# Sums of values over both key chunks in one visit of TensorE, with a re-measured planner

## The chip, the cores and the metric

The kernel runs on one core of a Trainium2 chip. Its engines are TensorE (PE in the profile; its weight loads are PEld), VectorE (DVE), ScalarE (ACT), GpSimd (POOL) and SyncE (SP), which issues all DMAs here. The metric is the device time of one execution in microseconds; a figure for a kernel is the median of its runs.

## The reference

Four transformer blocks follow each other on x, 16 batches of 256 tokens of width 256, with a context of 77 tokens a batch and a conditioning vector a batch. All is in fp32, with 16 heads of width 16.

```python
x = L0(x, cond, ctx, masks)   # adaLN, rope, masked self-attention, masked cross-attention, GELU MLP of 1024
x = L1(x, ctx, cond)          # adaLN on x and on ctx, cross-attention
x = L2(x, cond, ctx)          # adaLN, self-attention, cross-attention, MLP
x = L3(x, cond, ctx)          # adaLN, rope, self-attention, cross-attention, MLP

def attn(q, k, v, mask):      # in all of them
    s = einsum('bqhd,bkhd->bhqk', q, k) * scale      # masked in L0
    return einsum('bhqk,bkhd->bqhd', softmax(s), v)
```

So there are three self-attentions (256 keys, two chunks of 128), four cross-attentions (77 keys, one chunk) and three MLPs, each over 16 batches.

## The kernel before

**Stages.** All of x stays in SBUF. The work comes in stages: attention of L0 ("a" self, "ac" cross), its MLP ("b"), attention of L1 and L2 ("cx", "c", "cc"), its MLP ("d"), attention of L3 ("e", "ec"), its MLP ("f"). Within a stage the batches overlap in a wave: a batch's cross-attention starts 16 places behind its self-attention.

**One attention** (`attention`, L757). x is normed (`norm_tasks`: statistics on VectorE, scaling on POOL), turned through DRAM (a VectorE transpose of 32x32 blocks, L539, a DMA out, a DMA in) into xT; the first BY_PE = 2 batches of the masked attention are turned on TensorE instead (L518). Projections (`strips`, L639) cut the array into four column strips, 128 rows by 32 columns each. Heads lie in pairs of 32 rows: scores cut the array into four row strips, 32 by 128. There are two rounds of scores. In the first (L872 with 256 keys, L884 with 77) queries are on the partitions and VectorE takes each row's maximum from PSUM (L902, L906; for the masked self-attention with the mask added, L898; for the first BY_PE batches the mask is added by a bf16 matmul, L863). The maxima go through DRAM into the queries as extra rows. In the second round (L965, L958 the masks) keys are on the partitions; ScalarE takes the exponential of each bank (L979, L977) into a buffer "ec" of four row strips. One half (g) of the heads and one chunk (kc) of 128 keys fill one such buffer with four exponentials. Then `values` (L983, matmul L988) multiplies them with v in four column strips: eight matmuls a chunk, two visits of the array for a half in self-attention, both into one PSUM bank, which the first visit takes. v's tile holds 64 columns for a pair of heads, of which values fill two quarters and ones the other two, so that the same matmul sums the exponentials. The sums are turned by VectorE (L997), inverted (L1004), multiplied in by POOL (L1010), turned back (L1014) and projected (L639 again) onto x.

**The MLP** (`mlp`, L1065). Per batch eight blocks of 128 hidden units, two full-array matmuls each (L1087), GELU on ScalarE (L1092) into an "ec" buffer, and L1038 back. GELU and exponential need different function tables on ScalarE.

**Context.** `context_T` (L591) loads the context in ten tiles, norms it for L1 and L2, and turns it on TensorE (L626) into a buffer "ctx" of [2, 1232] columns. There are two such buffers; at the start one holds the bf16 masks. For L1, `scale1` (L1250) applies the modulation "1k" to the whole context on VectorE. A modulation (`modulation`, L379) loads weights into a "kq" buffer, multiplies (L389), turns (L400) and adds.

**Order.** Nothing is ordered by hand. Each step is a Task with an engine, an estimated duration, dependences, and the buffers (Hold) it takes and uses; CAPS says how many of each there are (8 PSUM banks "b", 2 "ec", 2 "ctx", 5 "kq", ...). `Order.solve` (L102) plays a list schedule on these estimates and returns the order in which the steps are issued. An engine takes the ready step of the least priority value (TensorE) or the longest ready one (the others); a result is taken to reach another engine LAG = 0.13 us after the step's end; a change between row strips and others costs 0.2 or 0.13 us (TURN). Two score steps of opposite halves of the rows (rp 0 and 1) are issued interleaved, so that all four row strips run; `choose` (L151) pairs them. Only the order depends on these estimates; on the chip the engines wait for semaphores.

The planner's constants and its one call, before:

```python
    LAG = 0.13                                                                   # L77
    u.ready = max(u.ready, t.end + (self.LAG if u.eng != t.eng else 0.0))        # L199
    for ts in od.solve():                                                        # L1302
```

Of the kernel before, what the change touches and what calls it, by code (L numbers as in the profile page):

```python
# [17 lines left out]
P = 128  # L18
# [55 lines left out]
class Order:  # L74


    LAG = 0.13  # L77
# [8 lines left out]
    def add(self, eng, dur, run, deps=(), take=(), use=(), prio=0, rp=None, kind=None, more=0.0,  # L86
            lat=0.0, first=False, mb=0.0):

        t = Task()
        t.more, t.lat, t.first, t.mb = more, lat, first, mb  # L90
# [9 lines left out]
        return t  # L100

    def solve(self, seed=0):  # L102
# [65 lines left out]
        while n_done < len(self.tasks):  # L168
# [19 lines left out]
            assert nxt, "no step can start"  # L188
            now = min(nxt)
            while events and events[0][0] <= now + 1e-9:  # L190
                _, _, t = heapq.heappop(events)
                n_done += 1
                for h in t.held:
                    h.users -= 1
                    if not h.users:
                        loose[h.tag].append(h.no)
                for u in t.outs:
                    u.left -= 1
                    u.ready = max(u.ready, t.end + (self.LAG if u.eng != t.eng else 0.0))  # L199
                    if not u.left:  # L200
                        waiting.setdefault(u.eng, []).append(u)
# [4 lines left out]
def pixart_kernel(ctx: ExitStack, tc: tile.TileContext, x, cond_t, ctx_in, mask_c, mask_s, tables, vecs, rows,  # L206
# [7 lines left out]
    CAPS = {"b": 8, "xn": 1, "xT": 2, "kq": 5, "v": 5, "mx": 3, "mr": 2, "ec": 2,  # L214
            "ts": 2, "oT": 2, "rope": 2, "qk": 4, "tmp": 2, "gb": 3, "wa": 1, "ctx": 2,
# [3 lines left out]
    wpool = ctx.enter_context(tc.tile_pool(name="weights", bufs=1))  # L219
# [5 lines left out]
    SHAPES = {"kq": [2, 2, 512], "v": [NT, H, 32], "xn": [NT, D], "xT": [NC, N], "y": [4, NT * NC * 32],  # L225
# [36 lines left out]
    h_mask = Hold("ctx")  # L262
# [31 lines left out]
    BY_PE = 2  # L294
# [5 lines left out]
    def ones_out():  # L300
        for m in mrs:
            nc.sync.dma_start(m[1].rearrange("s r n -> r s n"),
                              vs[-1][0:4].rearrange("r t h w -> r (t h w)").rearrange("r (s n) -> r s n", n=512))
    ones_t = add("POOL", 3.2, ones, prio=3)
# [34 lines left out]
    sc_t = add("DVE", 0.6, silu, deps=[t], prio=200)  # L339


    def load_weights(src, block, deps=(), prio=-1):
# [12 lines left out]
        h, views, tasks, s = Hold("wa"), {}, {}, {}  # L355

        def open_w():
            s["w"] = wpool.tile([P, WMAX], F32, tag="wa", name=f"w_{block}")
        t0 = add("NO", 0.0, open_w, deps=deps, take=[h], prio=prio)
        names, off = [], 0  # L360
        for name, cols in BLOCKS[block]:
            if name not in ("qr", "kr", "cqr", "ckr"):
                names.append((name, off, NC * cols))
            off += NC * cols

        def load(name, off, n):
            w = s["w"][:, off:off + n]
            nc.sync.dma_start(w, src[:, off:off + n])
            views[name] = w.rearrange("p (c n) -> p c n", c=NC)
        for i, (name, off, n) in enumerate(names):  # L370
            tasks[name] = add("SP", ISSUE, lambda name=name, off=off, n=n: load(name, off, n), deps=[t0],
# [123 lines left out]
    def norm_tasks(s, b, eps, mod, name, prio, deps=(), direct=False):  # L495
# [31 lines left out]
        t1 = add("DVE", 1.0, stats, deps=[x_done[b], *deps], take=[hs], prio=prio)  # L527
        t2 = add("POOL", 0.95, rstd, deps=[t1], use=[hs], prio=prio)
        t3 = add("POOL", 2.5, scale, deps=[t2], take=[hn], use=[hs], prio=prio)
# [32 lines left out]
        t = add("DVE", 0.75, turn32, deps=[t3], take=[hy], use=[hn], prio=prio)  # L562
# [28 lines left out]
    def context_T(name, eps, prio, deps=()):  # L591
# [6 lines left out]
        for j in range(0, CT, P):  # L598
# [7 lines left out]
            if eps is not None:  # L606
# [11 lines left out]
                t = add("DVE", 0.5, stats, deps=[t], take=[hs], use=[hi], prio=prio)  # L618
                t = add("POOL", 0.95, rstd, deps=[t], use=[hs], prio=prio)
# [31 lines left out]
    def take_q(s, bias, src, a, use, prio):  # L651
# [8 lines left out]
        return add("ACT", 1.1 if bias is None else 1.25, run, deps=[a], use=use, prio=prio)  # L660

    def take_k(s, bias, n, src, a, use, prio):
# [15 lines left out]
        d = (0.6 if big else 0.33) if bias is None else (0.95 if big else 0.5)  # L678
# [3 lines left out]
    def rotate_tasks(s, key, ws, xT, src_t, n, half, uses, name, prio):  # L682
# [6 lines left out]
        for group in ([list(range(nt))] if len(ws) == 1 else [[t] for t in range(nt)]):  # L689
# [44 lines left out]
            d = add("POOL", 0.65 * size, sines, deps=[a, tab_t], take=[hr], use=[hq], prio=prio)  # L734
# [22 lines left out]
    def attention(b, name, n, wv, wkeys, h_w, w_t, eps, mod, half, biases, masked, pre_add, gate, prio, ctxs=None,  # L757
# [7 lines left out]
        h_masks = [h_mask] if masked else []  # L765
# [68 lines left out]
        def take_v():  # L834
            pv = uv["p"][0:rows_n, 0:nk * D].rearrange("p (t h w) -> p t h w", h=H, w=HD)
            pairs = s["v"][0:rows_n, 0:nk].rearrange("p t (h i) w -> p t h (i w)", i=2)
            pairs = pairs.rearrange("p t h (a w) -> p t h a w", w=HD)
            for t in range(nk):
                nc.scalar.copy(pairs[:, t, :, 0:4:3, :], pv[:, t].rearrange("p (h i) w -> p h i w", i=2))
        a = add("PE", nk * NC * MM, mmv, deps=[*src_t, w_t[kv]], take=[hm3], kind="col" if self_ else None, use=[h_v, *h_src, *h_w], prio=prio)  # L840
        v_t = add("ACT", 0.37 * nk, take_v, deps=[a, ones_t], use=[hm3, h_v], prio=prio)
# [9 lines left out]
        for g in range(NC):  # L851
            for t in tiles:
                for rp in range(2):
# [3 lines left out]
                    def begin(g=g, t=t, rp=rp, u=u, hs=hs):  # L857
# [8 lines left out]
                        for i in range(2):  # L866
# [25 lines left out]
                            use=[h_kq, h_mx, *h_masks], prio=prio, rp=rp, kind="m")  # L892
                    for i in range(2):
# [15 lines left out]
                        red.append(add("DVE", 0.95 if self_ and masked and not by_pe else 0.69 if self_ else 0.46, reduce, deps=[a], use=[hs[i], h_mx],  # L909
# [24 lines left out]
        for g in range(NC):  # L934
            u5, avs, h_av, h_so = {}, [], Hold("b"), Hold("ts")
            for kc in range(nk):
# [8 lines left out]
                for rp in (1, 0):  # L945
# [3 lines left out]
                    def begin(g=g, kc=kc, rp=rp, u=u, hs=hs):  # L949
# [11 lines left out]
                        for i in range(2):  # L961
# [9 lines left out]
                    a = add("PE", 2 * MM, begin, more=0.26 if self_ and masked else 0.0,  # L971
                            deps=[t_e, k_t, *(mask_ts[self_][1] if masked else [])], take=hs, use=[h_kq, *h_masks], prio=prio, rp=rp, kind="e")
# [10 lines left out]
                def values(g=g, kc=kc, u5=u5, h_av=h_av):  # L983
                    u5["n"] = u5.get("n", 0) + 1
                    u5["p"] = psum(h_av, 2)
                    for q in range(2):
                        for r in range(4):
                            nc.tensor.matmul(u5["p"][32 * r:32 * r + 32, 1 - q, :],  # L988
                                             lhsT=s["v"][0:rows_n, kc, 8 * g + 2 * r + 1 - q, :],
                                             rhs=s["e", g, kc, r][0:rows_n, q, :],  # L990
                                             start=(u5["n"] == 1 and q == 0), stop=(u5["n"] == nk and q == 1))
                avs.append(add("PE", 2 * MM, values, deps=ex, take=[h_av],
                           use=[h_v, h_e], prio=prio, kind="col"))
# [415 lines left out]
```

## Time and profile before

| | |
|---|---|
| median of 3 runs | 2606.72 us (2603.66 to 2607.87) |
| the profiled execution | 2611.79 us |
| its span | 2610.0 us |
| TensorE, VectorE, ScalarE, POOL busy | 98%, 59%, 52%, 49% |
| granted TensorE clock over the span | 0.994 |
| matmuls recorded | 29112 |
| L979 exponentials | 1152 of 596 ns |
| L988 values | 5120 matmul records of 383 ns |
| L997 transposes of the sums | 224 of 708 ns |
| function-table loads on ScalarE | 18 of 1283 ns |

The profiled execution lasted 1.8 us longer than its span and 5.1 us longer than the median. An fp32 matmul is recorded as two. A group's line in the profile has: source line, engine, operation, out<-in, shapes, count | busy us, mean ns of one | idle us of the engine just before, and who ended it. A line of waits has: who waits, for whom, us in total, how often, the longest. PEclk is the granted TensorE clock.

### The profile page before, as it was taken

The page shows a single profiled execution, that of the slowest core. Times are in us where ns is not written, and L with a number is a line of the kernel's source. Part 1 is how long each engine was busy: PE and PEld are TensorE (multiplying, and loading weights), DVE is VectorE, ACT ScalarE, POOL GpSimd, SP SyncE. Part 2 cuts the span into 40 slices and gives each one's busy share as a digit, 9 for nine tenths or more (in the row PEclk, how much of TensorE's full clock was granted, in tenths as well). Part 3 has the DMA queues.
Part 4 walks back from the last instruction along what each step waited for, and adds up shares of the span by engine and source line. Part 5 has one row for each costly group of instructions (what it writes and reads, how often), then busy time and mean ns, then how long its engine had stood idle before and what let it go on. Part 6 is the DMA issues. An engine that isn't in the chain of part 4 may idle for free.

```text
span 2610.0 us, 71673 instructions
## 1 busy us (share of the span) xinstructions
PE 2550.0 (98%) x29112; PEld 1660.2 (64%) x29112; DVE 1550.4 (59%) x4265; ACT 1351.2 (52%) x2677; POOL 1276.9 (49%) x1653
## 2 busy tenths in 40 slices
PE   8999999999999899999999999999999999999999
PEld 4555555555888556555556556888555555556888
DVE  6877876776130577777777774111777777885100
ACT  3555655656233456565556565233565665555322
POOL 6455554558462355333335566433454455778210
PEclk9999999999999999999999999999999999999999
DMA  5101111223321121111111123111100001122110
GB/s 170 34 28 30 34 33 38 70 77 93 122 71 53 40 71 52 50 57 42 40 41 46 55 79 105 63 61 41 37 28 29 28 28 37 47 66 72 55 55 29
DMA packets 159811, 144.08 MB, mean 55 GB/s; under 512 B 24649, under 2 KB 124217, under 8 KB 158713
## 3 DMA queue, kind: packets, MB, share of 16 engines
q1 hardware_dynamic: 159480, 139.51, 17.1%
q8 instruction: 228, 3.74, 0.6%
q14 instruction: 103, 0.84, 0.1%
HBM read 91.86 MB, written 47.61 MB: 53 GB/s over the span
## 4 chain that ended last, share of the span: by engine, by line
PE 91%; DVE 3%; POOL 2%; ACT 2%; DMA 1%; issue 1%; SPq 0%; ACTq 0%; DVEq 0%; POOLq 0%
PE bank L639 22%; PE bank L965 13%; PE bank L1087 13%; PE bank L1038 12%; PE bank L988 11%; PE bank L872 8%; PE bank L831 2%; PE bank L884 2%; PE bank L648 2%; PE bank L958 2%; PE bank L752 2%; ACT ec L979 1%; POOL xn L511 1%; DVE mx L906 1%; DMA xr<-yd 1%
## 5 line engine op out<-in xcount | busy, mean ns | idle before, releaser
L979 ACT ACTIVATE ec<-bank 128x512 f32<-128x512 f32 (+1 forms) x1152 | 608.5, 596 | 401.7 <-PE bank L872 253.5
L965 PE MATMUL bank<-kq 32*128 32x256 f32 (+1 forms) x5120 | 631.6, 394 | 1.1 <-DVE mx L902 0.6
L511 POOL TENSOR_SCALAR xn<-x_sb,mv,rstd 128x256 f32<-128x256 f32 x320 | 457.9, 1485 | 106.2 <-DVE y L539 97.5
L965 PEld LDWEIGHTS bank<-kq 32*128 32x128 f32 (+1 forms) x5120 | 358.1, 167 | 179.2 <-issue 97.8
L872 PE MATMUL bank<-kq 32*128 32x512 f32 x1536 | 436.0, 633 | 1.2 <-ACT ec L979 1.0
L902 DVE TENSOR_REDUCE mx<-bank 128x2 f32<-128x512 f32 x544 | 340.7, 680 | 75.4 <-PE bank L872 74.4
L1092 ACT ACTIVATE ec<-bank,vec 128x256 f32<-128x256 f32 x384 | 159.6, 466 | 371.9 <-PE bank L1087 309.6
L988 PE MATMUL bank<-ec,v 128*32 128x256 f32 (+1 forms) x5120 | 346.0, 383 | 3.0 <-ACT ec L977 1.4
L1087 PE MATMUL bank<-xT,kq 128*128 128x256 f32 x1536 | 346.6, 382 | 0.4 <-ACT xT L559 0.4
L1038 PE MATMUL bank<-kq,ec 128*128 128x256 f32 x1536 | 341.5, 380 | 0.0
L1087 PEld LDWEIGHTS bank<-xT,kq 128*128 128x128 f32 x1536 | 290.2, 191 | 49.0 <-issue 8.3
L1038 PEld LDWEIGHTS bank<-kq,ec 128*128 128x128 f32 x1536 | 290.7, 190 | 42.0 <-issue 3.0
L539 DVE STREAM_TRANSPOSE y<-xn 128x512 f32<-128x512 f32 x158 | 110.5, 700 | 304.8 <-DMA yd<-y 244.7
L1010 POOL TENSOR_TENSOR od<-ts,rec 128x128 f32<-128x128 f32 x448 | 172.5, 406 | 241.6 <-DVE rec L1004 241.2
L988 PEld LDWEIGHTS bank<-ec,v 128*32 128x32 f32 (+1 forms) x5120 | 155.1, 110 | 150.2 <-issue 37.6
L906 DVE TENSOR_REDUCE mx<-bank 128x4 f32<-128x308 f32 x512 | 211.2, 467 | 47.8 <-PE bank L965 32.9
L898 DVE CUSTOM_DVE_ANT_0 junk<-bank,ctx 128x256 f32<-128x256 f32 x448 | 189.2, 422 | 56.7 <-PE bank L872 27.3
L997 DVE STREAM_TRANSPOSE ts<-bank 128x512 f32<-128x512 f32 x224 | 158.6, 708 | 96.6 <-PE bank L988 80.2
L722 POOL TENSOR_TENSOR rope<-qk,tabT 128x256 f32<-128x256 f32 (+2 forms) x224 | 135.0, 627 | 139.3 <-ACT qk L708 129.0
L486 POOL TENSOR_SCALAR rstd<-mv 128x2 f32<-128x2 f32 x160 | 37.6, 235 | 304.2 <-DVE mv L481 216.3
L884 PE MATMUL bank<-kq 32*128 32x154 f32 x2048 | 167.1, 306 | 2.3 <-DVE mx L906 0.8
L1059 POOL TENSOR_TENSOR x_sb<-x_sb,tmp 128x512 f32<-128x512 f32 x80 | 101.8, 1273 | 134.3 <-DVE tmp L1054 132.9
(167 smaller groups left out, 3405.9 us busy)
## 6 DMA issues: line engine op xcount, KB each, us to landing
yd<-y SPq DMA_DIRECT2D x158, 256.0 KB
xr<-yd SPq DMA_DIRECT2D x158, 256.0 KB
kq<-in_mod_dram SPq DMA_DIRECT2D x10, 512.0 KB
cin<-in_ctx_in_dram SPq DMA_DIRECT2D x36, 128.0 KB
x_sb<-in_x_dram SPq DMA_DIRECT2D x16, 256.0 KB
gb<-gate_g0m SPq DMA_DIRECT2D x16, 256.0 KB
gb<-gate_g2a SPq DMA_DIRECT2D x16, 256.0 KB
gb<-gate_g2m SPq DMA_DIRECT2D x16, 256.0 KB
```

Source lines behind the costliest of these rows:

```text
L511: nc.gpsimd.tensor_scalar(to, of, s["mv"][:, t, 0:1], s["rstd"][:, t:t + 1], ALU.subtract, ALU.mult)
L639: nc.tensor.matmul(dst[J], lhsT=l[:, J], rhs=r, start=(k == 0), stop=(k == len(pairs) - 1))
L872: ls.append(lambda ps=ps, R=R, keys=keys: nc.tensor.matmul(ps.rearrange("p (s k) -> p s k", k=N), lhsT=s["qx"][R, 0, g, t * P:(t + 1) * P] ...
L884: ls.append(lambda ps=ps, R=R, keys=keys, tt=tt: nc.tensor.matmul(ps[:, 2 * tt * n:2 * (tt + 1) * n].rearrange("p (s k) -> p s k", k=n), l ...
L898: nc.vector.tensor_tensor_reduce(junk, u[i][:, i2 * N:(i2 + 1) * N], mb[:, t, :], -1.0, 3.0e38, ALU.add, ALU.min, m[:, i2, g, t:t + 1])
L902: nc.vector.tensor_reduce(m[:, :, g, t], u[i].rearrange("p (s k) -> p s k", k=N), AX.X, ALU.max, negate=True)
L906: nc.vector.tensor_reduce(m[:, :, g].rearrange("p s t -> p t s"), u[i][:, 0:4 * n].rearrange("p (t s k) -> p t s k", s=2, k=n), AX.X, ALU. ...
L965: (lambda ps=u[i], R=R, q=q: nc.tensor.matmul(ps[0:rows_n, q * N:(q + 1) * N], lhsT=s["kz"][R, q, g, kc * P:kc * P + rows_n], rhs=s["qx"][ ...
L979: nc.scalar.activation(e, u[i][0:rows_n], AF.Exp)
L988: nc.tensor.matmul(u5["p"][32 * r:32 * r + 32, 1 - q, :], lhsT=s["v"][0:rows_n, kc, 8 * g + 2 * r + 1 - q, :], rhs=s["e", g, kc, r][0:rows ...
L1038: nc.tensor.matmul(u["p"][:, t, :], lhsT=lhsT(k, t), rhs=w()[:, k, :], start=(k == 0), stop=(k == nk - 1))
L1087: nc.tensor.matmul(u["p"][:, j, :], lhsT=wv["w1"][:, k, f * P:(f + 1) * P], rhs=s["xT"][:, k, :], start=(k == 0), stop=(k == NC - 1))
```

## The change

- `values` becomes one step for both chunks: sixteen matmuls in one visit instead of two visits of eight. It takes the bank for the sums only then, and both buffers of exponentials until its end.
- "ec" has four buffers instead of two (the MLP's hidden units use the same ones).
- v has 48 columns for a pair of heads, value, ones, value; a matmul takes columns 0 to 31 or 16 to 47.
- "ctx" has one buffer. The masks move to the unused end of the weights' tile, which is now a fixed tile; the weights of a block lie in it without the holes of the turned ones. The context of L2 is prepared later (priority `count[0] + 220`), since it needs L1's buffer.
- BY_PE is 1: batch 1 of the masked self-attention is turned through DRAM and masked on VectorE.
- The planner: LAG is 0.28 us behind TensorE and 0.08 otherwise; VectorE, ScalarE and POOL give AFTER (0.08, 0.13, 0.04 us) of a step's duration back to their own queue and add it to the result's delay; many estimated durations are set anew; thirteen orders are planned, twelve of them with random changes of TensorE's priorities, and the one with the shortest plan is taken.

```diff
-    LAG = 0.13
+    LAG = {"PE": 0.28}
+    AFTER = {"DVE": 0.08, "ACT": 0.13, "POOL": 0.04}
...
+        over = self.AFTER.get(eng, 0.0)
+        dur, lat = dur - over, lat + over
...
+    def best(self, n):
+
+        spans = []
+        for seed in range(n):
+            if self.solve(seed) is not None:
+                spans.append((max(t.end for t in self.tasks), seed))
+        return self.solve(min(spans)[1])
...
-            assert nxt, "no step can start"
+            if not nxt:
+                return None
...
-                    u.ready = max(u.ready, t.end + (self.LAG if u.eng != t.eng else 0.0))
+                    u.ready = max(u.ready, t.end + (self.LAG.get(t.eng, 0.08) if u.eng != t.eng else 0.0))
...
-    CAPS = {"b": 8, "xn": 1, "xT": 2, "kq": 5, "v": 5, "mx": 3, "mr": 2, "ec": 2,
-            "ts": 2, "oT": 2, "rope": 2, "qk": 4, "tmp": 2, "gb": 3, "wa": 1, "ctx": 2,
+    CAPS = {"b": 8, "xn": 1, "xT": 2, "kq": 5, "v": 5, "mx": 3, "mr": 2, "ec": 4,
+            "ts": 2, "oT": 2, "rope": 2, "qk": 4, "tmp": 2, "gb": 3, "wa": 1, "ctx": 1,
...
-    SHAPES = {"kq": [2, 2, 512], "v": [NT, H, 32], "xn": [NT, D], "xT": [NC, N], "y": [4, NT * NC * 32],
+    SHAPES = {"kq": [2, 2, 512], "v": [NT, H // 2, 48], "xn": [NT, D], "xT": [NC, N], "y": [4, NT * NC * 32],
...
-    BY_PE = 2
+    BY_PE = 1
...
-            pairs = s["v"][0:rows_n, 0:nk].rearrange("p t (h i) w -> p t h (i w)", i=2)
+            pairs = s["v"][0:rows_n, 0:nk].rearrange("p t h (a w) -> p t h a w", w=HD)
...
-                def values(g=g, kc=kc, u5=u5, h_av=h_av):
-                    u5["n"] = u5.get("n", 0) + 1
-                    u5["p"] = psum(h_av, 2)
+                h_es.append(h_e)
+                avs += ex
+
+            def values(g=g, u5=u5, h_av=h_av):
+                u5["p"] = psum(h_av, 2)
+                for kc in range(nk):
                     for q in range(2):
                         for r in range(4):
                             nc.tensor.matmul(u5["p"][32 * r:32 * r + 32, 1 - q, :],
-                                             lhsT=s["v"][0:rows_n, kc, 8 * g + 2 * r + 1 - q, :],
+                                             lhsT=s["v"][0:rows_n, kc, 4 * g + r, HD * (1 - q):HD * (1 - q) + 32],
                                              rhs=s["e", g, kc, r][0:rows_n, q, :],
-                                             start=(u5["n"] == 1 and q == 0), stop=(u5["n"] == nk and q == 1))
-                avs.append(add("PE", 2 * MM, values, deps=ex, take=[h_av],
-                           use=[h_v, h_e], prio=prio, kind="col"))
+                                             start=(kc == 0 and q == 0), stop=(kc == nk - 1 and q == 1))
+            avs = [add("PE", 2 * nk * MM, values, deps=avs, take=[h_av], use=[h_v, *h_es], prio=prio, kind="col")]
...
-    mask_b = mask_t.rearrange("p c n -> p (c n)")[:, 0:1408].bitcast(BF16)
+    mask_b = wa_t[:, 2 * 256 * 8:2 * 256 * 8 + 1408].bitcast(BF16)
...
-    c2 = context_T("2", 1e-6, p0)
+    c2 = context_T("2", 1e-6, count[0] + 220)
...
-    for ts in od.solve():
+    for ts in od.best(13):
```

Left out are the other edits of estimated durations and the packing of the weights in `load_weights`.

## The prediction

> **What bounds the kernel now.** I read the page's busy shares and its chain first, then stretches of TensorE's timeline, then the waits by engine.
>
> ```profile
> PE 2550.0 (98%) x29112; PEld 1660.2 (64%) x29112; DVE 1550.4 (59%) x4265; ACT 1351.2 (52%) x2677; POOL 1276.9 (49%) x1653
> ...
> PE 91%; DVE 3%; POOL 2%; ACT 2%; DMA 1%; issue 1%; SPq 0%; ACTq 0%; DVEq 0%; POOLq 0%
> ```
>
> TensorE is the bound: 98% busy, 91% of the chain that ended last. But a matmul's end is modelled and matmuls overlap, so "busy" hides lost time. Starts do not. This is TensorE's timeline in the middle block (start, length):
>
> ```profile
> 1231.76 1.93 PE L639 MATMUL bank<-w_c,oT 128*32 128x256 f32 x32
> 1233.51 1.05 PE L988 MATMUL bank<-ec,v 128*32 128x256 f32 x16
> 1234.48 0.48 PE L965 MATMUL bank<-kq 32*128 32x256 f32 x2
> 1234.50 0.70 PE L872 MATMUL bank<-kq 32*128 32x512 f32 x2
> ...
> 1235.55 1.93 PE L639 MATMUL bank<-xT,w_c 128*32 128x256 f32 x32
> ```
>
> L639 and L988 cut the array into four column strips (128*32), L965 and L872 into four row strips (32*128). The 32 matmuls of L639 are eight steps of four at once: 1233.51 - 1231.76 = 1.75 us, or 0.219 us a step. The visit of L988 is four steps, 0.88 us, but took 0.97 until the row strips began; the row work is four steps too and took 1.07 until the next columns. So a change of cut costs 0.09 to 0.19 us, 0.15 on average. The built order has 1,258 such changes. Laid end to end at 0.219 us a step (0.216 for full-array passes), the matmuls take about 2,240 us; the changes take about 190 more. The other 170 of the 2,610 us are waits, of which only some 50 show as gaps over 0.3 us; the rest are short. They are read from what TensorE's weight loads, which lead the matmuls, waited for:
>
> ```profile
> PEld bank L639 <- ACT ec L979: 29.4, 64, 2.6
> PEld bank L872 <- ACT ec L979: 23.5, 48, 0.8
> PEld bank L988 <- ACT ec L979: 13.5, 32, 1.2
> ```
>
> (microseconds, times, longest). TensorE waits for exponentials: to get a bank back (L872, L639) or to have the values' right-hand side (L988). It is a matter of order, not of ScalarE's speed, since ScalarE idles 48% of the time. The long gaps have a place each; the largest pair is this:
>
> ```profile
> 866.81 1.93 PE L639 MATMUL bank<-xT,w_c 128*32 128x256 f32 x32
> 869.33 1.89 PE L389 MATMUL bank<-kq,scondT 128*16 128x512 f32 x4 [0.58 <-DMA kq<-in_mod_dram]
> 871.94 0.42 PE L400 MATMUL bank<-ident,tmp 16*128 16x16 f32 x4 [0.72 <-ACT tmp L394]
> 877.32 0.71 PE L648 MATMUL bank<-ctx,w_c 128*128 128x77 f32 x2 [4.96 <-DVE ctx L1253]
> 880.30 1.56 PE L648 MATMUL bank<-ctx,w_c 128*128 128x77 f32 x6 [2.27 <-DVE ctx L1253]
> ```
>
> The scale and shift "1k" of the context is computed (L389, L400) only after the last MLP batch; VectorE then spends four steps of 1.4 to 1.6 us on it (L1252, L1253) while TensorE has nothing.
>
> **The change part by part.** All numbers are on the profiled execution, 2,611.8 us with a span of 2,610.0; the median of the runs is 2,606.7, so 5.1 us are taken off at the end. What moved was read from the two built orders.
>
> 1. Masks of batch 1 leave TensorE (BY_PE 2 to 1): 16 bf16 matmuls at 0.24 us (timeline: four of L863 from 49.31 to 50.28) are 3.8 us, and four transposes 0.6 us a batch (21.75 to 22.34). With the overlap of a change of cut counted below: -4.0 us. VectorE gets 32 custom reductions of 0.42 us with 32 read-outs of 0.08 (16 us) for 16 plain ones of 0.68 (11 us): +5 us at a place where it is 66 to 80% busy. Cover: TensorE's own work on batches 0 and 1; without it 5 us.
> 2. One visit for both key chunks. Each of the 96 (batch, block, half) of self-attention had two visits of eight matmuls, now one of sixteen: 319 visits become 224 in the built order. The same matmuls run, so only changes of cut are saved; and most single visits already stood beside other column work (180 of 319 followed some). Column blocks fall from 415 to 379, row blocks rise from 491 to 499, all changes fall from 1,258 to 1,231. This count includes ten context tiles of block 2 that now cut into attention. 27 x 0.15 = -4 us. The title's edit by itself is worth little.
> 3. The stall after the first MLP. In the new order the modulation "1k" stands 17 us of TensorE work behind "1q", inside the MLP, not after it, and the transposes of c2 leave this place for the attention (one context buffer, later priority). The gaps were 0.58 + 0.72 + 4.96 + 2.27 and one of 0.48 behind them, 9.0 us. The clock then stood at half:
>
> ```profile
> 878.00:882.00 4.00, 1.73 (x8) 1.61 (x8) 2.61 (x3) 1.19 (x3) 3.92 (x3) 0.50 0.01 3
> ```
>
>    (the third number from the end is PEclk), and the work there ran slow: eight of L648 took 2.3 us against 1.0 later, four of L831 1.9 against 1.1, eight of L648 1.4 against 1.0, together 2.4 us. -11.4 us, if nothing else is late at that place; the next would be the normed x through DRAM (7.3 us of ScalarE's waits there are for it), but in the new order that may start as before.
> 4. Values that came too early. I measure how much TensorE work lies between the last scores matmul and the visit that needs its exponential. Under 1.3 us (two exponentials of 0.6 plus about 0.1 to start are 1.3): 34 of 319 visits before, 9 of 224 after; under 2.0 us: 166 before, 44 after. The 34 match the 32 waits of L988 above. Of 13.5 us, 25/34: -10 us. The 0.28 us that the planner now gives TensorE's results to arrive does this; two more buffers of exponentials make it possible, as a visit holds two.
> 5. Banks asked back too early. Under 0.9 us of TensorE work between writing a bank and writing it again, with a ScalarE read between: 59 times before, of which 40 are L872 behind an exponential, twice a batch in the later blocks; 18 after (11 of that kind). The 48 waits of L872 are these, 0.49 us each: 41 x 0.49 = -20 us. From 0.9 to 1.3 us there are more than before (180 against 110 on ScalarE, 72 against 120 on VectorE); there a bank is just free, and I take it at nothing, between +5 and -5.
> 6. Start. Batch 1's x now goes through DRAM. Batch 2's trip in the trace took 27.83 to 35.11, 7.3 us from the transpose to xT; batch 1's xn is ready at 18.2, so its xT at 25.5 to 26 (SP's queue has the write ahead of the last twelve loads of x, the read behind two of them and two small loads). TensorE gets there at about 24: +2 us, bounds 0 and 6.
> 7. ScalarE's function tables: 26 loads for 18, all at the three ends of attention, where exponentials and GELUs interleave. Weighed against a rule of the Trainium skill:
>
> ```profile
> 614.97 0.84 ACT L1092 ACTIVATE ec<-bank,vec 128x256 f32<-128x256 f32 x2 [3.12 <-PE bank L1087]
> 615.83 1.28 ACT L977 ACT_TABLE_LOAD   x1
> 617.12 2.41 ACT L977 ACTIVATE ec<-bank,kbT 77x512 f32<-77x512 f32 x4
> ```
>
>    "ScalarE: Activation LUTs", section "What ACT_TABLE_LOAD costs", gives 1.28 us for the load and a drain of about 1.38, 2.66 us for a switch. Here work stands directly before and behind the load, and the drain isn't to be seen. Eight more cost ScalarE 10.3 us by the row and 21.3 by the rule; I take the row. MLP matmuls cover most of it (ScalarE is 32 to 43% busy there): +3 us on the path, bounds 0 and 10, and 21 without cover by the rule.
> 8. At nothing: v of 48 columns (the same 32 weight columns a load, the same copies; the fill of ones on POOL, 4.5 us at the start, gets a quarter shorter, bounds -1 and 0), masks in the spare part of the weights' tile (the block uses 4,096 of 6,144 columns, the masks 1,408 behind them), other planned durations except through the order.
>
> Sum: -4.0 - 4.0 - 11.4 - 10 - 20 + 2 + 3 = -44.4 us. 2,611.8 - 44.4 - 5.1 = 2,562 us.
>
> **The rivals.**
>
> *Eight exponentials behind one visit: slower.* A visit now waits for the last of eight exponentials, and TensorE's queue behind it waits too: the scores of the next pair, and so ScalarE itself. If ScalarE is a few exponentials behind its plan, every one of 96 visits waits. Without item 4's gain the sum is -34; from 34/96 = 0.36 us a visit on, the kernel is slower. An exponential lasts 0.6 us, so one more in the queue is enough. At 0.5 us a visit: 2,606.7 - 34 + 48 = 2,620 us. A rule speaks for it: the Trainium skill, "TensorEngine Tiling (Array Packing)", section "PSUM Bottleneck", says that cutting the array speeds up TensorE but not the emptying of PSUM, which may then bound. By it the 44 us saved on TensorE would be worth nothing. The row of attention speaks against:
>
> ```profile
> 1060.00:1160.00 100.00, 97.34 (x1422) 56.70 (x1421) 75.77 (x161) 59.86 (x122) 34.18 (x48) 1.00 0.17 51
> ```
>
> TensorE 97, VectorE 76, ScalarE 60 of 100 us: there is room for a late exponential, and three quarters of the two-chunk visits stand over 2.0 us behind their last scores.
>
> *Only what is counted.* The order of the other waits is reshuffled and the short waits come back elsewhere: the weight loads' 29.4 us for L639 show that a relieved place hands on its wait. Items 1 and 2 stay, items 3 to 5 are given back but for the costs: 2,606.7 - 8 + 3 = 2,602, with half of item 3 kept 2,596 us.
>
> *More than counted.* If the better lags also remove a third of the roughly 100 us of short waits left, another -33: 2,529 us.
>
> **How the numbers follow.** Forecast case (2,540 to 2,590) 0.60, more than counted 0.05, only counted 0.15 (of which 0.05 within 0.2%), slower 0.20. About 0.2%, 5 us, is what a measurement here can tell from no change. So faster 0.75, same 0.05, slower 0.20. The range: from 2,528 (items 4 and 5 and the rest at their best) to 2,612; beyond that some 0.15 of the slow case and 0.03 below.
>
> **What would show it.** Item 3: no gap of over 2 us before the first cross scores of block 1 and full clock there. Items 4 and 5: the weight loads of values and of L872's successor wait for exponentials less than half as long (13.5 and 23.5 us). Item 6: a gap before batch 1's first projection. Item 7: 26 loads of 1.28 us. Wrong, if TensorE's waits for exponentials grow in the stretches of self-attention; then the first rival holds.

## The result

| | before | changed kernel |
|---|---|---|
| median, us | 2607.30 (2603.66 to 2609.45, 4 runs) | 2590.64 (2586.27 to 2590.86, 4 runs) |
| ratio, 95% interval | | 0.9928 [0.9916, 0.9941] |
| profiled execution, its span, us | 2611.79, 2610.0 | 2590.76, 2589.0 |
| granted TensorE clock over that span | 0.994 | 0.990 |

The change makes the kernel 17 us faster, 0.7%. The forecast was 44 us, so the direction held and the size did not: less than half came. The profiled span fell by 21.0 us.

### The profile page after: what moved, and what is told of

Same layout as the page of the kernel before. It is cut to its first block, busy times and chain, and to the rows that moved or that the text cites. A ratio compares the mean times of both kernels' runs of the same rounds, so it can differ in the third digit from the quotient of the medians.

```text
span 2589.0 us, 71036 instructions
## 1 busy us (share of the span) xinstructions
PE 2532.3 (98%) x29092; PEld 1663.0 (64%) x29092; DVE 1550.2 (60%) x4314; ACT 1360.4 (53%) x2685; POOL 1273.0 (49%) x1653
## 3 DMA queue, kind: packets, MB, share of 16 engines
q1 hardware_dynamic: 160152, 140.03, 17.4%
## 4 chain that ended last, share of the span: by engine, by line
PE 86%; DVE 4%; DMA 3%; POOL 3%; ACT 2%; issue 1%; SPq 0%; DVEq 0%; ACTq 0%; POOLq 0%
PE bank L649 21%; PE bank L973 13%; PE bank L1048 13%; PE bank L1097 13%; PE bank L999 10%; PE bank L880 7%; PE bank L840 2%; DMA xr<-yd 2%; PE bank L892 2%; PE bank L966 2%; PE bank L762 2%; PE bank L658 1%; DMA yd<-y 1%; DVE mx L914 1%; POOL xn L521 1%
## 5 line engine op out<-in xcount | busy, mean ns | idle before, releaser
L973 PE MATMUL bank<-kq 32*128 32x256 f32 (+1 forms) x5120 | 631.0, 394 | 3.1 <-DVE mx L914 1.3
L521 POOL TENSOR_SCALAR xn<-x_sb,mv,rstd 128x256 f32<-128x256 f32 x320 | 451.7, 1466 | 117.3 <-DVE y L549 101.0
L973 PEld LDWEIGHTS bank<-kq 32*128 32x128 f32 (+1 forms) x5120 | 365.4, 167 | 180.4 <-issue 88.3
L880 PE MATMUL bank<-kq 32*128 32x512 f32 x1536 | 417.0, 632 | 1.4 <-DVE kq L687 1.0
L910 DVE TENSOR_REDUCE mx<-bank 128x2 f32<-128x512 f32 x528 | 330.4, 681 | 55.3 <-PE bank L880 52.9
L999 PE MATMUL bank<-ec,v 128*32 128x256 f32 (+1 forms) x5120 | 325.2, 383 | 5.6 <-ACT ec L987 3.2
L649 PE MATMUL bank<-wa,xT 128*32 128x256 f32 x4096 | 250.3, 386 | 1.5 <-ACT xT L569 1.3
L999 PEld LDWEIGHTS bank<-ec,v 128*32 128x32 f32 (+1 forms) x5120 | 161.6, 110 | 137.1 <-ACT ec L987 15.9
L906 DVE CUSTOM_DVE_ANT_0 junk<-bank,wa 128x256 f32<-128x256 f32 x480 | 202.3, 422 | 49.9 <-PE bank L880 18.4
L649 PE MATMUL bank<-wa,oT 128*32 128x256 f32 x3584 | 220.7, 385 | 3.6 <-DVE oT L1024 2.9
L649 PEld LDWEIGHTS bank<-wa,xT 128*32 128x32 f32 x4096 | 122.4, 111 | 109.2 <-issue 17.3
```

The source lines that it names most:

```text
L521: nc.gpsimd.tensor_scalar(to, of, s["mv"][:, t, 0:1], s["rstd"][:, t:t + 1], ALU.subtract, ALU.mult)
L649: nc.tensor.matmul(dst[J], lhsT=l[:, J], rhs=r, start=(k == 0), stop=(k == len(pairs) - 1))
L880: ls.append(lambda ps=ps, R=R, keys=keys: nc.tensor.matmul(ps.rearrange("p (s k) -> p s k", k=N), lhsT=s["qx"][R, 0, g, t * P:(t + 1) * P] ...
L906: nc.vector.tensor_tensor_reduce(junk, u[i][:, i2 * N:(i2 + 1) * N], mb[:, t, :], -1.0, 3.0e38, ALU.add, ALU.min, m[:, i2, g, t:t + 1])
L910: nc.vector.tensor_reduce(m[:, :, g, t], u[i].rearrange("p (s k) -> p s k", k=N), AX.X, ALU.max, negate=True)
L973: (lambda ps=u[i], R=R, q=q: nc.tensor.matmul(ps[0:rows_n, q * N:(q + 1) * N], lhsT=s["kz"][R, q, g, kc * P:kc * P + rows_n], rhs=s["qx"][ ...
```

## The profile after, beside the one before

The page's busy row and its chain:

```profile
PE 2532.3 (98%) x29092; PEld 1663.0 (64%) x29092; DVE 1550.2 (60%) x4314; ACT 1360.4 (53%) x2685; POOL 1273.0 (49%) x1653
...
PE 86%; DVE 4%; DMA 3%; POOL 3%; ACT 2%; issue 1%; SPq 0%; DVEq 0%; ACTq 0%; POOLq 0%
```

TensorE is still the bound, but its share of the chain went from 91 to 86%: more of the end is now set by others. What TensorE's weight loads waited for (us in all, times, longest):

```profile
PEld bank L649 <- ACT ec L987: 30.1, 81, 1.2
PEld bank L973 <- ACT ec L987: 19.1, 56, 1.6
PEld bank L999 <- ACT ec L987: 15.9, 30, 2.6
...
PEld bank L880 <- ACT ec L987: 7.4, 28, 0.7
PEld bank L999 <- ACT ec L985: 6.3, 12, 2.3
```

Two rows of the kernel before to set beside these:

```profile
PEld bank L965 <- ACT ec L979: 7.0, 23, 0.6
PEld bank L988 <- ACT ec L977: 3.8, 7, 1.6
```

L649 is the old L639 (projections), L880 the old L872 (first scores), L973 the old L965 (second scores), L999 the old L988 (values). The first scores' wait fell from 23.5 to 7.4 us, as forecast. The values' wait did not fall: 13.5 us, with 3.8 more behind L977, became 15.9 and 6.3. The second scores' wait rose from 7.0 to 19.1. All weight-load waits for exponentials together were 95.4 us and are 91.7. So in total this wait was hardly removed; it shows at other places.

The stall after the first MLP did go. These are the same steps as in the forecast's item 3 (L399 the old L389, L658 the old L648), and the clock there (third number from the end of the second block):

```profile
861.46 1.11 PE L658 MATMUL bank<-ctx,wa 128*128 128x77 f32 x8
862.51 1.89 PE L399 MATMUL bank<-kq,scondT 128*16 128x512 f32 x4
```

```profile
855.00:865.00 10.00, 10.00 (x99) 6.78 (x97) 4.19 (x10) 3.23 (x7) 5.36 (x4) 1.00 0.01 2
```

No idle is noted before them, and the clock is at 1.00 where it was 0.50. But two stalls are new. One is at the end of the attention of L2 (start, length, step, idle before it and who ended it):

```profile
1539.15 1.19 PE L636 MATMUL bank<-ident,cin 128*128 128x128 f32 x4 [2.54 <-DMA cin<-in_ctx_in_dram]
1540.27 1.94 PE L999 MATMUL bank<-ec,v 77*32 77x256 f32 x16
...
1546.49 1.07 PE L999 MATMUL bank<-ec,v 77*32 77x256 f32 x16
1547.49 0.81 PE L892 MATMUL bank<-kq 32*128 32x154 f32 x16
1552.31 1.09 PE L636 MATMUL bank<-ident,cin 128*128 128x128 f32 x4 [4.01 <-DMA cin<-in_ctx_in_dram]
```

L636 turns the tiles of the context of L3. They now need the one "ctx" buffer, whose last reader for L2 (L840) runs at 1523.98, and the trace has the first of these loads at that same 1523.98. Before, the second buffer let all ten tiles pass earlier, inside the attention (L626, from 1074.1 to 1161.7). The other stall is at the end of the attention of L3:

```profile
2329.75 2.50 PE L999 MATMUL bank<-ec,v 77*32 77x256 f32 x32 [0.41 <-ACT ec L987]
2337.97 5.51 PE L1097 MATMUL bank<-xT,kq 128*128 128x256 f32 x16 [5.72 <-ACT xT L569]
```

The first MLP step stands in TensorE's queue ahead of work that was ready, and its input is still on its way through DRAM (VectorE's transpose ends at 2330.4, xT's first copy starts at 2337.32).

Both stalls have half clock beside them (again the third number from the end):

```profile
1540.00:1546.00 6.00, 6.00 (x50) 3.40 (x52) 2.31 (x9) 1.98 (x5) 4.90 (x9) 0.50 0.37 74
2335.00:2341.00 6.00, 3.03 (x7) 2.49 (x8) 4.17 (x15) 2.37 (x3) 5.92 (x9) 0.50 0.37 117
```

In the first of them the sixteen records of L999 took 1.94 us, and 1.07 at 1546.49, after it; the kernel before has full clock in both stretches. So the time lost there is more than the idle time.

To add this up I split each span by matmul starts into three: the matmuls laid end to end; the changes of cut, each at its usual cost in these traces (0.14 us from columns to rows, 0.21 back); and the rest, "lost", by stage. The first row is a count at one rate: it falls because fewer matmuls run.

| us | before | after | difference |
|---|---|---|---|
| matmuls end to end | 2210.8 | 2206.9 | -4 |
| changes of cut | 193.5 | 187.7 | -6 |
| lost after the first MLP | 15.1 | 4.2 | -11 |
| lost in the middle of the three attentions | 136.2 | 113.8 | -22 |
| lost at the start | 15.7 | 19.9 | +4 |
| lost at the end of the attention of L1 and L2 | 8.9 | 17.4 | +9 |
| lost at the end of the attention of L3 | 5.4 | 14.9 | +10 |
| the rest | 24.4 | 24.2 | 0 |

Unrounded, the differences make the 21.0 us. Work done at half clock is in "lost". In the half-clock stretches at the end of the attention of L1 and L2 there are matmuls that would take 4.4 us at full clock (none before), at that of L3 6.8 us (1.8 before). If they took twice as long, some 9 of the 18 us that these two ends lost more are the clock; this is an estimate.

## The experiments

All ratios are to the kernel before, on the same chip. Differences in us between two runs can be across chips; on these the kernel before measured 2607.3 to 2610.4.

**The two halves of the change.** My theory after the result was that the structure gives what the forecast counted and the new planner takes part of it away. The rivals: the structure itself gives little, or the pick among thirteen orders carries the gain (theory B in the expectations).

e1_seed0 and e2_seed7 take one order instead of the best of thirteen, e2 the one that the planner rates worst (`od.solve(7)` in the line of e1):

```diff
-    for ts in od.best(13):
+    for ts in od.solve():
```

> The changed kernel with the first of its thirteen orders (no random change of TensorE's priorities) in place of the one it picked. Theory A (the structure and the measured lags made the gain, the pick among orders is small): within 5 us of the changed kernel, 2586 to 2596 us. Theory B (the order is a lottery, and picking the best of thirteen made most of the 17 us): 2598 to 2610 us, near the kernel before.

Measured: 2603.90 us, 0.9987 [0.9974, 1.0001].

> The changed kernel with another of its thirteen orders, the one that its own planner rates worst. Theory A (the pick is small): 2588 to 2600 us. Theory B (the pick is most of it): slower than the kernel before, 2608 to 2620 us.

Measured: 2605.55 us, 0.9995 [0.9985, 1.0005]. The pick is worth 13 us; without it nearly nothing is left of the gain. But the order rated worst is no slower than the unchosen one, so here the planner's rating says little about a single order. In e1 the place after the first MLP lost 11.5 us again, so item 3's gain comes neither with the structure nor with the new planner's estimates; e2, which was not picked, has no wait of TensorE there at all (840 to 895 us; 4.8 us in e1). It is a property of the single order.

e3_plan_only is the kernel before with the new LAG, AFTER, durations and `best(13)`; e4_struct_only is the changed kernel with the planner of before:

```diff
-    LAG = {"PE": 0.28}
-    AFTER = {"DVE": 0.08, "ACT": 0.13, "POOL": 0.04}
+    LAG = 0.13
...
-        t = add("DVE", 0.71, turn32, deps=[t3], take=[hy], use=[hn], prio=prio)
+        t = add("DVE", 0.75, turn32, deps=[t3], take=[hy], use=[hn], prio=prio)
...
-    for ts in od.best(13):
+    for ts in od.solve():
```

(with all other durations of before.)

> The kernel before with the planner of the changed one alone: lags, delays behind an engine's step, the new durations and the best of thirteen orders; two visits for the values, two buffers of exponentials, two context buffers, masks of two batches on TensorE. If the planner is what brings the gain: 2588 to 2597 us. If the structure is what brings it: 2602 to 2608 us. Its order has 1,314 changes of cut against 1,258 before (56 x 0.15 = 8 us more), so that a small loss is possible too, up to 2612.

Measured: 2608.52 us, 0.9998 [0.9988, 1.0007].

> The changed kernel with the planner of before: one lag of 0.13 us, no delays, the old durations, one order. If the structure brings the gain: 2586 to 2597 us; its order has 1,197 changes of cut, 61 fewer than before, 9 us, and 4 us of masks, and only 11 banks asked back too early. If the planner brings it: 2603 to 2615 us.

Measured: 2567.34 us, 0.9847 [0.9833, 0.9862]. The structure alone gives 41 us, and the new planner brings nothing to the kernel before and takes 23 us from the structure. The stretch that the forecast looked at, in e4:

```profile
1060.00:1160.00 100.00, 100.00 (x1454) 59.72 (x1449) 83.79 (x185) 61.82 (x127) 41.77 (x62) 1.00 0.17 53
```

That is 1,454 matmul records in 100 us, against 1,422 before and 1,390 in the changed kernel; but such a count depends on which work falls into the stretch. e4's weight loads waited 98.3 us for exponentials, more than before, though it is the faster one. Where it gained by the split: lost time in the middle of the attentions -34 us, changes of cut -11, matmuls -4. The place after the first MLP still lost 13.6 us, so e4 has the 41 us without item 3.

**Which part of the planner.** Theory L blamed the lags, theory D the durations. e5 is e4 with the new lags alone (below), e6 is e4 with the new durations alone, such as the 0.71 above.

```diff
-    LAG = 0.13
+    LAG = {"PE": 0.28}
+    AFTER = {"DVE": 0.08, "ACT": 0.13, "POOL": 0.04}
```

> The changed structure with the planner of before (2567 us), and of the new planner only the lags: 0.28 us behind TensorE, 0.08 behind others, and the delays behind a step. Theory L (the longer lags make the planner cut the work finer, and each change of cut costs): its order has 1,303 changes of cut against 1,197, 106 x 0.15 = 16 us, so 2580 to 2595 us. Theory D (the new durations do the harm): 2563 to 2572 us.

Measured: 2577.34 us, 0.9883 [0.9869, 0.9898].

> The changed structure with the planner of before, and of the new planner only the twenty or so new durations. Its order has 1,206 changes of cut, 9 more than without them, 1 us, and 30 banks asked back too early for 11. Theory L: 2565 to 2578 us. Theory D: 2585 to 2605 us.

Measured: 2582.96 us, 0.9900 [0.9884, 0.9917]. Neither theory alone holds: the lags cost 10 us and the durations 16. The lags' 10 us fits the changes of cut: the built order has 1,303 against 1,197, and the split puts 16 us more there. The durations leave the changes of cut nearly as they were (1,206) and lose 16 us more by the split (21 in the attention of L1 and L2, 9 in that of L3, 14 less elsewhere).

e7 and e8 take other orders of e4, e7 the one of the thirteen that its planner rates worst, e8 the pick (`od.best(13)` in the line of e7):

```diff
-    for ts in od.solve():
+    for ts in od.solve(4):
```

> The changed structure with the planner of before, in another order: TensorE's priorities changed at random by the fourth seed, which the planner itself rates worst of the first thirteen. If the 41 us of that structure are a property of it: 2570 to 2592 us, still clearly below the kernel before. If its one order was a lucky draw: 2595 to 2615 us.

Measured: 2634.43 us, 1.0100 [1.0085, 1.0115].

> The changed structure with the planner of before, and of the new one only the pick of the best of thirteen orders. The pick gained 13 us with the new lags (2604 to 2591). Theory A (the planner's rating holds on the chip with either lags): 2548 to 2560 us, a version that beats both kernels clearly. Theory B (with the short lag the rating says little): 2562 to 2585 us.

Measured: 2563.21 us, 0.9831 [0.9816, 0.9845], the fastest kernel of the study: it beats the one before by 1.7%, and the changed one too. e7 is the same program in another order, 67 us slower than e4, with only 1,161 changes of cut: fewer changes don't make a fast order when its waits grow (lost time 238 us against 166; the granted clock is 0.983 against 0.993). With the lags of before the rating did hold for these two: the order rated worst is the slowest, the pick the fastest.

e18_after_old_lags is the changed kernel with the lags of before, its durations and its pick kept:

```diff
-    LAG = {"PE": 0.28}
-    AFTER = {"DVE": 0.08, "ACT": 0.13, "POOL": 0.04}
+    LAG = 0.13
```

> The changed kernel with the lags of before (0.13 us everywhere, no delays), the new durations and the pick of thirteen kept. 1,204 changes of cut for 1,231, 4 us. If the lags do harm even with the pick: 2570 to 2584 us. If the pick makes up for them: 2586 to 2596 us.

Measured: 2566.79 us, 0.9833 [0.9817, 0.9850]. Without the new lags the kernel is 24 us faster. Here the changes of cut are only a small part of it (1,231 against 1,204, some 5 us); the rest is lost time. With the pick, the durations cost only 3.6 us (e18 against e8), not 16. In e18 the weight loads wait more for exponentials than in the kernel before or the changed one:

```profile
PEld bank L646 <- ACT ec L984: 40.2, 97, 1.7
...
PEld bank L996 <- ACT ec L984: 19.3, 33, 2.4
PEld bank L970 <- ACT ec L984: 16.8, 49, 0.4
```

(L646 projections, L996 values, L970 second scores), 113.8 us in all, 22 us more than the changed kernel, which is 24 us slower. So such a row is not a price: weight loads wait while matmuls ahead of them still run. In the kernel before their waits for exponentials alone are 95.4 us, and TensorE is idle for 60 of 2,610 us by the page.

**Which part of the structure.** All start from e4. e11 takes two buffers of exponentials; e9 makes two visits again, but still creates both steps after both chunks' scores; e10 is e9 with two buffers (the first edit below is that of e11 and e10, the second that of e9 and e10):

```diff
-    CAPS = {"b": 8, "xn": 1, "xT": 2, "kq": 5, "v": 5, "mx": 3, "mr": 2, "ec": 4,
+    CAPS = {"b": 8, "xn": 1, "xT": 2, "kq": 5, "v": 5, "mx": 3, "mr": 2, "ec": 2,
...
-            avs = [add("PE", 2 * nk * MM, values, deps=avs, take=[h_av], use=[h_v, *h_es], prio=prio, kind="col")]
+            avs = [add("PE", 2 * MM, lambda kc=kc, values=values: values(kc), deps=avs[4 * kc:4 * kc + 4], take=[h_av], use=[h_v, h_es[kc]], prio=prio, kind="col")
+                   for kc in range(nk)]
```

> The changed structure with the planner of before, one visit, but only two buffers of exponentials, which one visit holds both. Its order has 1,153 changes of cut, 44 fewer than with four, 7 us, but 107 banks asked back too early against 11, at 0.4 us 40 us. Theory E: 2595 to 2620 us. Theory M, buffers of no weight: 2555 to 2572 us.

Measured: 2685.96 us, 1.0297 [1.0282, 1.0313].

> The changed structure with the planner of before (2567 us), but two visits for the values again, each after its own four exponentials; four buffers of exponentials stay. Its order has 1,328 changes of cut against 1,197. Theory M (the one visit makes the gain, through changes of cut): 131 x 0.15 = 20 us more, 2582 to 2594 us. Theory E (the four buffers make it, since TensorE waits less): 2565 to 2575 us.

Measured: 2580.04 us (2570.38 to 2587.94), 0.9888 [0.9855, 0.9920].

> As the run with two visits, and two buffers of exponentials: that is the kernel before with its own planner, and of the change only the 48 columns, one context buffer and batch 1's masks on VectorE. 1,289 changes of cut against 1,258 before. Both theories: near the kernel before, 2598 to 2612 us; below 2592 the small edits would have made the gain.

Measured: 2579.82 us, 0.9885 [0.9869, 0.9902]. One visit with two buffers costs 119 us against e4, so here the merge cannot do without the buffers. Its waits for exponentials are 146.6 us, the most of all (L877 first scores):

```profile
PEld bank L877 <- ACT ec L984: 44.5, 102, 1.2
PEld bank L996 <- ACT ec L984: 37.8, 74, 1.8
```

With four buffers the merge is worth 13 us by the medians (e9 to e4), but e9's four runs lie in two pairs: 2570.38 and 2574.20 at granted clocks of 0.994 and 0.993, 2585.88 and 2587.94 at 0.988 and 0.987. e4's four are at 0.991 to 0.993. The first pair is 3 and 7 us slower than e4's median, and the traces (e9's is of the first pair) are 8 us apart: 131 fewer changes of cut, 20 us by the split, of which 12 come back as lost time. So at like clock the merge is worth 3 to 8 us. With two visits, two more buffers are worth next to nothing (e10). I had expected e10 near the kernel before, and it is 29 us faster. What is left there that differs is small edits, and where the two steps stand in the list of tasks: the planner breaks equal priorities by number, and a step made later loses ties. So e13 moves only that, in the kernel before (below); e14 and e15 are e9 and e10 with the steps made inside the loop, as in the kernel before:

```diff
+                later.append((values, ex, h_e))
...
+            for values, ex, h_e in later:
                 avs.append(add("PE", 2 * MM, values, deps=ex, take=[h_av],
```

> The kernel before with one thing changed: in the list of tasks the values of the two chunks stand behind the scores of both, so that at equal priority TensorE takes the second chunk's scores before the first chunk's values. No computation, buffer or estimate changes. Its order has 1,308 changes of cut for 1,258 (8 us more) and 26 banks asked back too early for 59. Theory P (this place is what the structure changed, by the way): 2580 to 2592 us. Theory S (the small edits, masks, one context buffer, 48 columns, are it): 2605 to 2615 us.

Measured: 2596.70 us, 0.9944 [0.9926, 0.9961].

> The changed structure with the planner of before and two visits, whose values stand in the list of tasks where the kernel before has them, each chunk's behind its own scores; four buffers of exponentials. Theory P: the gain of the two-visit kernel (2580 us) is lost, 2593 to 2606 us; theory S: 2575 to 2585 us.

Measured: 2596.71 us, 0.9950 [0.9935, 0.9965].

> The same with two buffers of exponentials: of the change only the small edits are left (48 columns, one context buffer, masks of batch 1 on VectorE). Theory P: 2598 to 2606 us, the kernel before less 4 us for the masks. Theory S: 2577 to 2585 us.

Measured: 2612.72 us, 1.0014 [1.0005, 1.0023]. The small edits alone (masks, v's 48 columns, context buffer, weights) give nothing or 4 us of loss. From there the structure's gain is a ladder: the later place in the list -33 (e15 to e10), four buffers 0 (to e9), one visit -13 (to e4). By the other way, four buffers first, they give 16 and the place 17. In the kernel before the place alone gives 12. The merge, which the title names, is the smaller step; the place in the list is the largest.

**How much is the order's chance?** One planned duration of a VectorE step moves by 0.04 us; nothing else changes. e12 does it in e4, e16 in the kernel before, and e17 in the changed kernel the other way, 0.71 to 0.75:

```diff
-        t = add("DVE", 0.75, turn32, deps=[t3], take=[hy], use=[hn], prio=prio)
+        t = add("DVE", 0.71, turn32, deps=[t3], take=[hy], use=[hn], prio=prio)
```

> The changed structure with the planner of before, and one of its estimated durations changed by 0.04 us (0.75 to 0.71 for a transpose), which makes another order with as many changes of cut (1,198) and the same count of banks asked back early (11). This shows how far two orders of equal quality lie apart by chance. If single orders can be compared: 2563 to 2572 us. If they scatter so that the 10 and 16 us of lags and durations mean nothing: outside 2559 to 2576.

Measured: 2568.82 us, 0.9847 [0.9832, 0.9862].

> The kernel before with one estimated duration changed by 0.04 us (0.75 to 0.71 for a transpose): another order of like quality, 1,277 changes of cut, 52 banks asked back too early. If the kernel before is no unlucky draw: 2600 to 2616 us. If it is: 2575 to 2595 us.

Measured: 2628.61 us, 1.0072 [1.0057, 1.0087].

> The changed kernel with one estimated duration changed by 0.04 us (0.71 to 0.75 for a transpose), thirteen orders planned and the best taken, as in it; 1,237 changes of cut for 1,231. If the 23 us that the new planner loses against the old one are real: 2583 to 2602 us. If they are the scatter of orders: anywhere between 2565 and 2582.

Measured: 2579.76 us, 0.9884 [0.9870, 0.9899]. These edits moved e4 by +1.5, the kernel before by +20, the changed one by -11 us. By the medians, then, differences below some 20 us between two single orders are not pinned to one edit.

Most of this scatter goes with the clock. A run's time multiplied by its granted clock is what it would have taken at full clock, if TensorE had work all through the half-clock stretches. This is an estimate: it takes off too much where TensorE idled in them, and the clock is given to 0.001, which is 2.6 us. e9 tests it: its four runs, 17.6 us apart, become 2556.2, 2555.0, 2554.3 and 2554.8. The medians of this, beside those measured:

| from, to | measured, us | at full clock, us (estimate) |
|---|---|---|
| null edit: before to e16, changed to e17, e4 to e12 | +20, -11, +1.5 | +5, 0, -3 |
| later place: before to e13, e15 to e10, e14 to e9 | -12, -33, -17 | -24, -33, -24 |
| four buffers, two visits: e15 to e14, e10 to e9 | -16, 0 | -12, -3 |
| one visit, four buffers: e9 to e4 | -13 | -6 |
| new lags: e4 to e5, e18 to changed | +10, +24 | +13, +15 |
| new durations: e4 to e6, e8 to e18 | +16, +4 | +11, -3 |
| structure alone: before to e4 | -41 | -42 |
| new planner with its pick: e4 to changed | +23 | +17 |
| orders of one program: e4 to e7, e1 to changed | +67, -13 | +38, -12 |

The null edits now lie within 5 us, though another random order still costs e4 38 us, and the place and the lags agree better from pair to pair. Beyond the scatter of the null edits are the structure, e11, the later place (24 to 33 us) and the lags (13 to 15). The merge's 6 us are hardly beyond it, though its 131 changes of cut are counted. The durations stay open. e9 shows that one program can be granted either clock, so it is not the order alone that sets it; what does is not shown by these runs.

## Why the forecast was right in direction and wrong in size

- **What failed.** On the profiled span -44.4 us were forecast and -21.0 came. By the split, 18 of the 23 us between them are the two ends of attention, which the sum had at nothing, and 8 are items 4 and 5, whose price was wrong (30 us forecast, 22 found). The other items nearly cancel.
- **Item 1, right.** Forecast -4.0; the matmuls end to end fell by 3.9 us, which is a count. What the 5 us more on VectorE cost was not isolated.
- **Item 2, right in its number, wrong in its reason.** The built order has 27 fewer changes of cut, as counted, and the split gives -6 us. But "the title's edit by itself is worth little" is wrong: with the old planner the merge removes 131 changes (e9, e4), though in time it is worth only 3 to 8 us at like clock. The later place in the list, which the same edit brings and the forecast did not consider, adds changes (1,308 against 1,258 in e13) and is worth more. The count of 27 is the sum of these and of the changes that the new lags and durations put in.
- **Item 3, right.** -10.9 us against -11.4, full clock, no gap. Its source is the single order, though: e1 and e4, which have no pick, lost 11.5 and 13.6 us there; e3, e8 and e18, which have it, 3.0 to 3.5; and e2, not picked, has no wait there either.
- **Items 4 and 5, wrong in price and reason.** They held 30 of the 44 us. Item 5's sum also takes all 41 relieved places at L872's 0.49 us, when only 29 of them are L872's; that is 14 us, and its row fell by 16. What failed is the price: a wait by weight loads taken as time of the kernel, and the wait from 0.9 to 1.3 us of distance taken at nothing. The rows of L973 and of the values took over, and all waits for exponentials fell by 3.7 us. Nor does the time follow them from kernel to kernel: e18 has more of them and is 24 us faster. The lost time in the attentions did fall by 22 us; by which waits is not shown. The sentence "The 0.28 us that the planner now gives TensorE's results to arrive does this" finds no support as a gain: the lags cost 10 us in e5, and without them e18 is 24 us faster. The estimate may be truer; with it the list schedule built more changes of cut (1,303 against 1,197 in e5, 1,231 against 1,204 with the pick). In e5 that accounts for the cost, in the changed kernel only for some 5 us; where its other lost time comes from stays open.
- **Item 6, nearly.** +4 against +2, inside its bounds. **Item 7:** 26 loads of 1,283 ns, as counted; no run isolates their cost, but e18 has the same 26 and takes 2567 us.
- **What was not in the sum at all:** the ends of the attentions of L2 and L3, +18 us, of which some 9 are half clock (estimate). The forecast saw that the tiles of one context now cut into attention, and took the single "ctx" buffer only as a help for item 3. What the buffer delays next was not asked: the context of L3, at the end of L2's attention. e4 has the single buffer too and lost only 9.0 us at that end, as much as before; its tiles there (from 1536.73 on) show no idle ahead of them. So this stall is the buffer and the order together. Time at the ends also comes and goes with the order alone: e13 and e16 keep both context buffers and wait there (1520 to 1600 us) 10.6 and 7.5 us, for other inputs. A run of the changed kernel with two context buffers was not made, and none isolates the stall at the end of L3.
- **The rivals.** *Only what is counted* (2,596 to 2,602) named the mechanism, a relieved place hands on its wait; the result lies 5 us below it, just above the forecast case's own stretch, which ended at 2,590. *Eight exponentials behind one visit* is half seen: the values' waits are longer (2.6 us the longest, 1.6 before), yet with four buffers the visit does not lose. With two buffers it is what happens (e11).

That e4's 41 us lie close to the forecast's 44 is luck: they come without item 3, and by the ladder mostly from the place of the values in the list of tasks, which the forecast did not have.

## What to carry to other kernels

Where a list scheduler writes the order, first measure what a null edit does (here -11 to +20 us of 2,600), set the granted clock of each run beside its time, and change structure and planner in separate runs: a truer estimate need not give a better order. Count changes of mode and waits apart in the built order, and price a wait by the starts of the engine's own work, never by a row of waits that may lie under running work. When a buffer is taken away, follow it to its next owner at the next stage's end. And look at what an edit does to the order of equal steps: here that was worth more than the edit itself.

## What was not expected of the hardware

The changes of cut do not cost the same both ways: by the starts, 0.14 us from columns to rows, 0.21 back. At 1,200 to 1,300 of them they are some 190 of 2,600 us, and the page counts that time as busy: e4's stretch above is busy for 100.00 of 100 us, changes of cut included, and TensorE shows 98% in the kernel before, in the changed one and in e18 alike, though the span of the first and the last differ by 44 us.

One program on one chip was granted mean clocks of 0.987 to 0.994 (e9), and its time went with them, by 17.6 us of 2,580.
